# Row sums of the last 128 queries' exponentials: from TensorE and POOL to ScalarE, in every second head group

## The chip, the cores and the metric

The kernel runs on one core of a Trainium2 chip. The core has five engines that run side by side, each with its own queue that it works off in order: TensorE (PE in the profile: matrix products into PSUM), VectorE (DVE), ScalarE (ACT: functions of one element, here exponentials and copies), GpSimd (POOL) and SyncE (SP), which issues nearly all DMAs. They wait for each other through semaphores. PSUM has eight banks of 128 partitions by 512 floats.

The metric is the device time of one execution, in microseconds (us). Before the change it is 815.91 us, the median of three runs (814.34 to 816.56).

## The reference

The input x has 16 sequences of 512 tokens with 128 features. Each sequence goes through three layers with residual sums: half a feed-forward, causal attention, half a feed-forward.

```python
x = x + 0.5 * ffn(layernorm(x))
x = x + attention(layernorm(x))
x = x + 0.5 * ffn(layernorm(x))
# attention: 16 heads, keys and values through a latent of 32 columns
attn = softmax(where(key <= query, q @ k.T / 8, -inf))     # per head, 512 x 512
y = attn @ v ; out = y @ Wout
```

The softmax is what the change touches: for each head and query, exponentials of scores less their maximum, and the sum of these exponentials by which the output is divided.

## The kernel before

**Folded weights.** The weights of queries and keys are multiplied together beforehand, and those of values and outputs too. A head's scores are then products over 32 latent columns. Four heads make a head group (`HG = 4`), and a sequence has four groups. Groups are worked on in pairs; u = 0 and u = 1 name the first and the second group of a pair. The kernel has 32 pairs.

**Blocks and kinds.** The 512 queries are four blocks of 128. Because of the causal mask, query block i needs keys 0 to (i+1) x 128. Work is cut into kinds: kind 0 is query block 3 (the last 128 queries, all 512 keys), kind 1 is blocks 2 and 0, kind 2 is block 1 of both groups.

**Two score passes.** Each score is computed twice. The first pass (tile `sx`, queries on partitions, keys along the row) only gives the maxima: VectorE takes the largest of each row with its sign turned (`find_maxima`, line 642, tile `nmax`). POOL splits the maxima into three bf16 terms (`maxima`), TensorE turns them (`maxima_t`, tile `mt`), ScalarE copies them (`rows`). The second pass (tile `tx`, keys on partitions, queries along the row) starts from these maxima, adds the scores, and ScalarE takes exponentials into SBUF (`exponentials`, line 655, tiles `pt`). POOL sets what the causal mask forbids to zero (`zeros`, line 668).

**Steps.** A pair takes five steps, n % 5 = 0 to 4, in the order `STEP = ((0, 0), (1, 0), (2, 0), (1, 1), (0, 1))` of (kind, u). So step 4 does the first pass of kind 0 of the second group: the last 128 queries. In each step `burst` (line 673) runs the first pass of the current pair and the second pass of work six steps older (`LAG`), in two halves of two heads each that `merge` interleaves. The first half's stream is tx of heads 0 and 1 followed by sx of heads 0 and 1; beside it run sx of heads 2 and 3 and then tx of heads 2 and 3.

**Between the bursts** come products that are due:

- `values` (line 763): probabilities by latent, tile `o`, in step 4 for u = 0 and in step 1 for u = 1. ScalarE copies it to `osb` (line 773).
- `sums` (line 781): the exponentials by a matrix of ones, tile `s`, in step 0 for u = 0 and in step 2 for u = 1. ScalarE copies it (`ssb`, line 787), four DMAs write it to DRAM, one reads it back spread over 128 partitions; VectorE takes reciprocals, DMAs broadcast them, and POOL multiplies them onto `osb` (`normalise`, line 830).
- Before `sums`, POOL adds the exponentials of equal queries over the key blocks, so that TensorE streams fewer columns: `add_01` (line 738, two instructions of 768 columns), `add_2` (line 743) and `add_23` (line 748, for the last 128 queries alone).
- Work of neighbouring sequences: `front` (feed-forward `fp_a`, layer norm, transposition, keys `kt`, queries `qt`) and `tail` (output products `yp`, second feed-forward `fp_c`).

**What sets the order.** The program order on every engine is written by hand. `FRONT_STEPS`, `SECOND_STEPS` and `TAIL_STEPS` (lines 509 to 513) say at which step, counted from the first burst of the sequence, each piece of `front` and `tail` is issued; a sequence lasts ten steps. A value n - 0.25 stands right behind burst n and ahead of `values` and `sums`; a value n stands behind them; n - 0.5 stands ahead of the burst.

The entries of `FRONT_STEPS` are in order: statistics (two), loads of the next x, bias, turning z, feed-forward, statistics (two), layer-norm scaling, blocks back from DRAM, turning, keys `kt`, `kt` to DRAM, `kt` from DRAM, and the four query products.

**PSUM.** Two pools: four single banks (`bank`, tag tx) and two double banks (`two_banks`, tag sx), each used in turn. A burst takes all four single banks for tx and both double banks for sx. The products between bursts take their output through `take` (line 74): single banks for the first two, a double bank for a third.

```python
between.extend((bank, bank, lambda name: two_banks(name)[:, 0, :]))
```

A bank that is taken again must first have been read by whoever reads its old content.

Of the kernel before, what the change touches and what calls it, by code (L numbers as in the profile page):

```python
# [11 lines left out]
F32 = mybir.dt.float32  # L12
BF16 = mybir.dt.bfloat16
AF = mybir.ActivationFunctionType
# [4 lines left out]
P = 128  # L19
# [6 lines left out]
def macaron_kernel(  # L26
# [14 lines left out]
    nc = tc.nc  # L41
    B, L, D = x.shape
    LD = wkv.shape[1]
# [5 lines left out]
    HG = P // LD  # L49
# [6 lines left out]
    small = ctx.enter_context(tc.tile_pool(name="small", bufs=6))  # L56
# [3 lines left out]
    dram = ctx.enter_context(tc.tile_pool(name="dram", bufs=4, space=bass.MemoryType.DRAM))  # L60
# [5 lines left out]
    def bank(name):  # L66
        return ps_t.tile([P, 512], F32, tag="tx", name=name)

    def two_banks(name):
        return ps_s.tile([P, 2, 512], F32, tag="sx", name=name)  # L70
# [3 lines left out]
    def take(name):  # L74

        return between.popleft()(name) if between else bank(name)
# [429 lines left out]

    FRONT_STEPS = (-31, -30.5, -29, -28, -21, -19.25, -16, -16, -13, -10.5, -8, -4.25, -4, -3.5, -2, -1, 3, 4)
    SECOND_STEPS = (-9.5, -8.5, -7, -5.5, -5, -4.25, -4, -3.5, -2, -1, 3, 4)  # L510
    THIRD_STEPS = (-18.5, -18.5, -18.5, -18, -17.5, -17.25, -16, -16) + FRONT_STEPS[8:]
    FOURTH_STEPS = (-27, -26, -25.5, -25) + FRONT_STEPS[4:]
    TAIL_STEPS = (1.75, 2.5, 2.75, 3.5, 4.5, 7, 7, 7.75, 10.5)
# [102 lines left out]
    def probabilities(st, g, kind):  # L616

        if ("pt", kind, g) not in st:
            st["pt", kind, g] = probs.tile(
                [P, 4, HG, P], F32, tag=f"pt{kind}", name=f"pt{kind}_{st['b']}_{g}", bufs=1 if kind == 2 else 2  # L620
            )
        return st["pt", kind, g]

    def merge(*streams):

        at = [0.0] * len(streams)
        streams = [deque(seq) for seq in streams]
        while any(streams):
            k = min((k for k in range(len(streams)) if streams[k]), key=lambda k: at[k])
            for _ in range(2):  # L630
                dst, w, mv, first, last = streams[k].popleft()
                nc.tensor.matmul(dst, lhsT=w, rhs=mv, start=first, stop=last, skip_group_check=True)  # L632
            at[k] += math.prod(mv.shape[1:]) * (1 if mv.dtype == BF16 else 4)

    def find_maxima(sx, st, g, kind, u, pair):
# [9 lines left out]
        else:  # L645
            nc.vector.tensor_reduce(  # L646
                nmax[:, 1, heads, :], sx.rearrange("p k (u n) -> p k u n", u=2), AX.X, ALU.max, negate=True
            )

    def exponentials(tx, st, g, kind, u, pair):  # L650

        pt = probabilities(st, g + (u if kind < 2 else 0), kind)
        if isinstance(tx, list):
            for k in range(2):
                nc.scalar.activation(  # L655
                    pt[:, :, 2 * pair + k, :], tx[k].rearrange("p (b n) -> p b n", n=P), AF.Exp
                )
        else:
            nc.scalar.activation(
                pt[:, :, ts(pair, 2), :].rearrange("p b k n -> p k b n"),  # L660
                tx.rearrange("p k (b n) -> p k b n", n=P), AF.Exp,
            )
# [10 lines left out]
    def burst(n, s_at, t_at):  # L673


        s_kind, t_kind = STEP[n % 5], STEP[(n - LAG) % 5]
        ss, tt, s_seq, t_seq = [], [], [], []
        for k in range(2):
            if t_at:
                tt.append([bank(f"tx_{t_at[0]['b']}_{t_at[1]}_{n}") for _ in range(2)])  # L680

                t_seq.append(t_parts(tt[k], *t_at, *t_kind, k, k == 0 and (n - LAG) % STEPS == 0))
            ss.append(two_banks(f"sx_{s_at[0]['b']}_{s_at[1]}_{n}"))
            s_seq.append(s_parts(ss[k], *s_at, *s_kind, 1 - k, t_at is not None and k == 1))
        if t_at:
            merge(t_seq[0] + s_seq[1], s_seq[0] + t_seq[1])
        else:
            merge(s_seq[0])
            merge(s_seq[1])
        for k in range(2):  # L690
            find_maxima(ss[k], *s_at, *s_kind, 1 - k)
            if t_at:
                exponentials(tt[k], *t_at, *t_kind, k)
        if n % STEPS == STEPS - 1:
            maxima(*s_at)
        if t_at:
            zeros(*t_at, *t_kind)
# [33 lines left out]

    def add_01(st, g, k):

        if k == 0:
            st["b01", g] = probs.tile([P, 3, HG, P], F32, tag="b01", name=f"b01_{st['b']}_{g}")
        flat = [t.rearrange("p b k n -> p (b k n)")[:, ts(k, 6 * P)] for t in (
            st["b01", g], st["pt", 0, g][:, 1:], st["pt", 1, g][:, 1:])]
        nc.gpsimd.tensor_tensor(*flat, ALU.add)  # L738

# [4 lines left out]

    def add_23(st, g, u):

        both = st["b23", g + u] = probs.tile([P, HG, P], F32, tag="b23", name=f"b23_{st['b']}_{g + u}")
        nc.gpsimd.tensor_tensor(both, st["pt", 2, g][:, 2 + u], st["pt", 1, g + u][:, 0], ALU.add)  # L748

    def blocks(dst, w, tile_, start=False):  # L750

        for h in range(HG):
            mv = tile_[:, :, h, :]
            nc.tensor.matmul(  # L754
                dst[ts(h, LD), :].rearrange("p (b n) -> p b n", n=P), lhsT=w[h] if isinstance(w, list) else w,
                rhs=mv, start=start, stop=True, skip_group_check=True,
            )
# [17 lines left out]
    def sum_products(st, g, u, s_ps):  # L775
        g1, w = g + u, ones_f[:, :LD]
        blocks(s_ps[:, :P], w, st["pt", 0, g1][:, :1], start=True)
        blocks(s_ps[:, P:], w, st["b01", g1])
        blocks(s_ps[:, 384:], w, st["b23", g1].unsqueeze(1))

    def sums(st, g, u):

        b, g1 = st["b"], g + u
        s_ps = take(f"s_{b}_{g1}")
        sum_products(st, g, u, s_ps)
        ssb = act2.tile([P, L], F32, tag="ssb", name=f"ssb_{b}_{g1}", bufs=3)
        nc.scalar.copy(ssb, s_ps)
        sums_d = dram.tile([HG, L], F32, tag="sums", name=f"sums_{b}_{g1}")
        for h in range(HG):
            nc.sync.dma_start(sums_d[h : h + 1], ssb[h * LD : h * LD + 1, :])  # L790
        st["sums", g1] = small.tile([P, HG * L // P], F32, tag="sum", name=f"sum_{b}_{g1}")
        nc.sync.dma_start(st["sums", g1], sums_d.rearrange("h n -> (h n)").rearrange("(p n) -> p n", p=P))

# [71 lines left out]
    groups = [(states[b], g) for b in range(B) for g in range(0, NG, 2)]  # L865
    N = len(groups)
    STEPS = len(STEP)
# [57 lines left out]
    def parts(when):  # L925
        gens = todo.pop(when, ())
        for gen in gens:
            next(gen)
        return bool(gens)
# [7 lines left out]
    plan(first, 0, (0, 3, 4))  # L937
    plan(second, WINDOW, SECOND_STEPS)
    plan(second_normalised(), 0, (1.75, 2))
# [4 lines left out]
    for b in range(2, B):  # L944
        plan(front(b, states[b]), b * WINDOW, {2: THIRD_STEPS, 3: FOURTH_STEPS}.get(b, FRONT_STEPS))
    for b in range(B - 2):
# [4 lines left out]
    def due(n, k, lag=LAG):  # L951

        at_ = at(n, lag + k)
        return at_ if at_ and (n - lag - k) % STEPS == 0 else None

    def turn_maxima(n):
        if due(n, STEPS, 0):
            maxima_t(*due(n, STEPS, 0))

    def ready_work(n):  # L960

        if n < N * STEPS and due(n, 10):
            st, g = due(n, 10)
            normalise(st, g + 1)
        for u in range(2):
            if due(n, 2 + 3 * u):
                st, g = due(n, 2 + 3 * u)
                add_01(st, g + u, 0)
                add_01(st, g + u, 1)
            if due(n, 3 + 2 * u):  # L970
                add_2(*due(n, 3 + 2 * u), u)
            if due(n, 3 + u):
                add_23(*due(n, 3 + u), u)

    for n in range(N * STEPS):
        parts(n - 0.5)
        ready_work(n)
        burst(n, at(n), at(n, LAG))
        if due(n, 8):
            normalise(*due(n, 8))  # L980
        if n >= LAG:
            between.extend((bank, bank, lambda name: two_banks(name)[:, 0, :]))

        parts(n - 0.25)
        for u in range(2):
            if due(n, 3 + 2 * u):
                values(*due(n, 3 + 2 * u), u)
            if due(n, 4 + 2 * u):
                sums(*due(n, 4 + 2 * u), u)
        turn_maxima(n)  # L990
        if not parts(n) and n < LAG:
            keep_clock(4)
        for u in range(2):
            if due(n, 6 + 2 * u):
                st, g = due(n, 6 + 2 * u)
                reciprocals(st, g + u)
        between.clear()
# [4 lines left out]
    n = N * STEPS  # L1002
# [25 lines left out]
    o_ps, s_ps = bank("o_late"), bank("s_late")  # L1028
# [75 lines left out]
```

## Time and profile before

| | |
|---|---|
| median of three runs | 815.91 us |
| the profiled execution | 814.67 us, of which the span is 812.9 |
| granted TensorE clock in it | 0.989 of full speed, mean |
| one pair of groups (five bursts, 400.87 to 425.68) | 24.8 us |
| exponentials on ScalarE, line 655, 128x512 | 616 instructions, 598 ns each |
| maxima on VectorE, line 642, 128x1024 | 128 instructions, 1223 ns each |
| copies osb and ssb on ScalarE | 62 each, 585 and 586 ns |
| POOL additions, lines 738 / 743 / 748 | 126 / 63 / 63, 1821 / 1277 / 1277 ns |

The profile gives the busy time of each engine, rows of instruction groups by line (out<-in, how often, mean length, idle time before them and who ended it), a table of waits, a timeline of each engine, and the chain of work that ended last. In a timeline row the first number is the start in us from the beginning of the span, the second how long the (merged) instructions took together, and a bracket at the end is idle time of the engine before it and who ended that. In the table of waits the numbers are: us in total, how many times, and (where shown) the longest.

### The profile page before, as it was taken

What the parts mean: (1) busy time and instruction counts of PE and PEld (TensorE: products, weight loads), DVE (VectorE), ACT (ScalarE), POOL (GpSimd) and SP (SyncE); (2) the same over time, 40 slices, a digit from 0 to 9 for tenths busy, and PEclk for the clock granted to TensorE, in tenths of its full rate; (3) what the DMA queues carried; (4) which work ended last, traced back from release to release, by engine and by line L of the source; (5) the groups of instructions that cost most, each with busy time, mean ns of one, the idle gap of its engine ahead of it and who ended that gap; (6) DMA issues with size and microseconds to landing.
All of it is one profiled execution on the core that took longest, in us unless ns stands there. A gap on an engine that the chain in (4) does not pass through costs nothing.

```text
span 812.9 us, 35716 instructions
## 1 busy us (share of the span) xinstructions
PE 786.7 (97%) x15400; PEld 506.9 (62%) x15400; DVE 618.6 (76%) x1317; ACT 488.9 (60%) x971; POOL 678.4 (83%) x676
## 2 busy tenths in 40 slices
PE   7899999999999999999999999999999999999986
PEld 5456566675666657666566766666666766666554
DVE  7787887978779687877869787777878677686716
ACT  1237675757567565756667566666757566575651
POOL 1018898998998999898989989898999989998991
PEclk9989999999999999999999999999999999999998
DMA  5123122232422323332232323223222222212111
GB/s 138 27 57 68 32 72 60 69 71 73 95 61 69 77 66 80 76 82 60 70 84 61 84 69 82 67 67 88 56 64 67 51 72 69 59 46 59 41 41 30
DMA packets 171022, 54.01 MB, mean 66 GB/s; under 512 B 119512, under 2 KB 162680, under 8 KB 170864
## 3 DMA queue, kind: packets, MB, share of 16 engines
q1 hardware_dynamic: 170096, 51.44, 27.1%
q8 instruction: 120, 1.97, 1.0%
q14 instruction: 38, 0.31, 0.1%
q10 hardware_dynamic: 768, 0.30, 0.1%
HBM read 37.90 MB, written 13.80 MB: 64 GB/s over the span
## 4 chain that ended last, share of the span: by engine, by line
PE 75%; POOL 7%; DVE 7%; ACT 4%; DMA 4%; issue 2%; SPq 1%; DVEq 0%; POOLq 0%
PE sx L632 18%; PE tx L632 14%; PE o L754 14%; PE s L754 8%; PE yp L385 7%; PE qt_ps L385 6%; POOL b L738 4%; DVE nmax L642 3%; PE fp_a L385 2%; DMA rb<-recs 2%; ACT xn_b L355 2%; PE fp_c L385 2%; POOL ot L830 1%; DMA recs<-rec 1%; POOL b L743 1%
## 5 line engine op out<-in xcount | busy, mean ns | idle before, releaser
L642 DVE TENSOR_REDUCE nmax<-sx 128x2 f32<-128x768 f32 (+2 forms) x384 | 313.0, 863 | 106.4 <-PE tx L632 66.0
L655 ACT ACTIVATE pt<-tx 128x512 f32<-128x512 f32 x616 | 319.5, 598 | 85.5 <-PE tx L632 79.3
L632 PE MATMUL sx<-kt,qt 32*128 32x512 f32 (+3 forms) x2048 | 324.5, 444 | 0.0
L632 PE MATMUL tx<-qt,kt 32*128 32x512 f32 x1728 | 319.3, 469 | 0.0
L738 POOL TENSOR_TENSOR b<-pt,pt 128x768 f32<-128x768 f32 x126 | 226.8, 1821 | 0.5
L632 PEld LDWEIGHTS sx<-kt,qt 32*128 32x128 f32 x2048 | 176.7, 186 | 25.1 <-issue 1.0
L668 POOL TENSOR_SCALAR_AFFINE_SELECT pt<-pt 128x1024 f32<-128x1024 f32 (+1 forms) x162 | 145.2, 900 | 24.1 <-ACT pt L655 21.0
L754 PE MATMUL o<-pt,lat 128*32 128x512 f32 x1984 | 146.4, 435 | 0.9 <-POOL pt L668 0.9
L632 PEld LDWEIGHTS tx<-qt,kt 32*128 32x128 f32 x1728 | 131.5, 185 | 5.1
L754 PEld LDWEIGHTS o<-pt,lat 128*32 128x32 f32 x1984 | 62.5, 109 | 78.0 <-issue 57.7
L632 PE MATMUL tx<-rows,ones_u 6*128 6x512 bf16 (+1 forms) x988 | 109.9, 297 | 1.0 <-DVE wvo L292 0.5
L646 DVE TENSOR_REDUCE nmax<-sx 128x4 f32<-128x1024 f32 x64 | 75.4, 1219 | 32.1 <-PE tx L632 32.0
L830 POOL TENSOR_TENSOR ot<-osb,rb 128x512 f32<-128x512 f32 x62 | 79.0, 1274 | 20.3 <-DMA rb<-recs 20.3
L632 PEld LDWEIGHTS <-ones_u 6*128 6x128 bf16 x1024 | 43.2, 92 | 82.8 <-issue 70.1
L773 ACT COPY osb<-o 128x512 f32<-128x512 f32 x62 | 36.3, 585 | 92.3 <-PE o L754 92.3
L632 PE MATMUL sx<-eye_b,mask_w 32*128 32x64 bf16 (+1 forms) x2560 | 87.8, 183 | 2.9 <-DVE nmax L646 1.9
L632 PEld LDWEIGHTS <-mask_w 32*128 32x128 bf16 x2560 | 67.4, 92 | 33.0 <-issue 25.1
L743 POOL TENSOR_TENSOR b<-b,pt 128x512 f32<-128x512 f32 x63 | 80.5, 1277 | 5.1
L748 POOL TENSOR_TENSOR b<-pt,pt 128x512 f32<-128x512 f32 x63 | 80.4, 1277 | 0.1
L487 ACT COPY qt<-qt_ps 128x512 f32<-128x512 f32 x64 | 37.5, 586 | 53.8 <-PE qt_ps L385 53.8
L754 PE MATMUL s<-b,ones_f 128*32 128x384 f32 x992 | 65.1, 380 | 3.5 <-POOL b L743 3.5
L385 PE MATMUL qt_ps<-xnt_b_b,wqk 128*32 128x512 f32 x512 | 68.2, 605 | 0.1
(193 smaller groups left out, 813.8 us busy)
## 6 DMA issues: line engine op xcount, KB each, us to landing
rb<-recs SPq DMA_DIRECT2D x248, 64.0 KB
x<-in_x_dram SPq DMA_DIRECT2D x16, 256.0 KB
sums<-ssb SPq DMA_DIRECT2D x248, 2.0 KB
z_a<-in_x_dram SPq DMA_DIRECT2D x60, 64.0 KB
blocks_b<-xn_b SPq DMA_DIRECT2D x15, 256.0 KB
z_b<-blocks_b SPq DMA_DIRECT2D x60, 64.0 KB
kt<-kt_d SPq DMA_DIRECT2D x60, 64.0 KB
out_dram<-x_c SPq DMA_DIRECT2D x15, 256.0 KB
```

What stands on the lines that cost most here:

```text
L385: nc.tensor.matmul(dst[ts(h, LD), :], lhsT=w[:, ts(h, LD)], rhs=mv, start=start, stop=stop, skip_group_check=True)
L487: nc.scalar.copy(st["qt", g - g % 2][:, g % 2, :], mp)
L632: nc.tensor.matmul(dst, lhsT=w, rhs=mv, start=first, stop=last, skip_group_check=True)
L642: nc.vector.tensor_reduce(nmax[:, i, heads, u], sx[:, :, col : col + (i + 1) * P], AX.X, ALU.max, negate=True)
L646: nc.vector.tensor_reduce(nmax[:, 1, heads, :], sx.rearrange("p k (u n) -> p k u n", u=2), AX.X, ALU.max, negate=True)
L655: nc.scalar.activation(pt[:, :, 2 * pair + k, :], tx[k].rearrange("p (b n) -> p b n", n=P), AF.Exp)
L668: nc.gpsimd.affine_select(diag, diag, pattern=[[0, diag.shape[1]], [1, P]], compare_op=ALU.is_ge, fill=0.0, base=0, channel_multiplier=-1,)
L738: nc.gpsimd.tensor_tensor(*flat, ALU.add)
L743: nc.gpsimd.tensor_tensor(b01, b01, st["pt", 2, g][:, u], ALU.add)
L748: nc.gpsimd.tensor_tensor(both, st["pt", 2, g][:, 2 + u], st["pt", 1, g + u][:, 0], ALU.add)
L754: nc.tensor.matmul(dst[ts(h, LD), :].rearrange("p (b n) -> p b n", n=P), lhsT=w[h] if isinstance(w, list) else w, rhs=mv, start=start, sto ...
L830: nc.gpsimd.tensor_tensor(turned(st)[:, g, :], st["osb", g], st["rb", g], ALU.mult)
```

## The change

In step 4, behind the exponentials of the burst, ScalarE now also works on the first-pass scores of the second group's last 128 queries, which are still in the double banks `sx`. For each of the four heads one instruction takes exp(score - maximum) in place over the 512 keys, with the negated maximum as a per-partition bias, and its accumulator output gives the sum over the row (tile `own`). This is done in all pairs but the last (31 of 32). A new DMA, at the start of the step 2 that follows, writes these 128 x 4 sums into the sums' place in DRAM.

For these groups, `add_01` covers 512 columns per instruction in place of 768, `add_23` is left out, the product with ones covers queries 0 to 383, the copy `ssb` and its DMAs too.

Besides, pieces of `front` are moved: the feed-forward from step 1 to step 4 (-19.25 to -21.25), the keys from step 1 to step 4 (-4.25 to -6.25), and the four query products from steps 3, 4, 3, 4 to steps 1, 3, 1, 3.

```diff
-    FRONT_STEPS = (-31, -30.5, -29, -28, -21, -19.25, -16, -16, -13, -10.5, -8, -4.25, -4, -3.5, -2, -1, 3, 4)
-    SECOND_STEPS = (-9.5, -8.5, -7, -5.5, -5, -4.25, -4, -3.5, -2, -1, 3, 4)
+    FRONT_STEPS = (-31, -30.5, -29, -28, -22, -21.25, -16, -16, -13, -10.5, -8, -6.25, -5.5, -4.5, -4, -2, 1, 3)
+    SECOND_STEPS = (-9.5, -8.5, -7, -5.5, -5, -4.25, -4, -3.5, -2, -1, 1, 3)
...
+    def own_sums(sx, st, g, pair):
+        if ("own", g + 1) not in st:
+            st["own", g + 1] = small.tile([P, HG], F32, tag="own", name=f"own_{st['b']}_{g}", bufs=3)
+        for k in range(2):
+            nc.scalar.activation(
+                sx[:, k, :], sx[:, k, :], AF.Exp, bias=st["nmax", g][:, 3, 2 * pair + k, 1:2],
+                accum_out=st["own", g + 1][:, 2 * pair + k : 2 * pair + k + 1],
+            )
+
+    def own_sums_out(st, g):
+        sums_d = st["sums_d", g + 1] = dram.tile([HG, L], F32, tag="sums_0", name=f"sums_{st['b']}_{g}", bufs=3)
+        nc.sync.dma_start(sums_d[:, 384:].rearrange("h q -> q h"), st["own", g + 1])
...
             find_maxima(ss[k], *s_at, *s_kind, 1 - k)
             if t_at:
                 exponentials(tt[k], *t_at, *t_kind, k)
+        if n % STEPS == STEPS - 1 and s_at is not groups[N - 1]:
+            for k in range(2):
+                own_sums(ss[k], *s_at, 1 - k)
...
     def add_01(st, g, k):
+        n_ = (4 if ("own", g) in st else 6) * P
...
-        flat = [t.rearrange("p b k n -> p (b k n)")[:, ts(k, 6 * P)] for t in (
+        flat = [t.rearrange("p b k n -> p (b k n)")[:, ts(k, n_)] for t in (
...
     def add_23(st, g, u):
+        if ("own", g + u) in st:
+            return
...
         blocks(s_ps[:, :P], w, st["pt", 0, g1][:, :1], start=True)
+        if ("own", g1) in st:
+            blocks(s_ps[:, P:384], w, st["b01", g1][:, :2])
+            return
         blocks(s_ps[:, P:], w, st["b01", g1])
         blocks(s_ps[:, 384:], w, st["b23", g1].unsqueeze(1))
...
-        nc.scalar.copy(ssb, s_ps)
-        sums_d = dram.tile([HG, L], F32, tag="sums", name=f"sums_{b}_{g1}")
+        n_ = 384 if ("own", g1) in st else L
+        nc.scalar.copy(ssb[:, :n_], s_ps[:, :n_])
+        sums_d = st["sums_d", g1] if n_ < L else dram.tile([HG, L], F32, tag="sums", name=f"sums_{b}_{g1}")
         for h in range(HG):
-            nc.sync.dma_start(sums_d[h : h + 1], ssb[h * LD : h * LD + 1, :])
+            nc.sync.dma_start(sums_d[h : h + 1, :n_], ssb[h * LD : h * LD + 1, :n_])
...
         parts(n - 0.5)
+        if due(n, STEPS + 2, 0):
+            own_sums_out(*due(n, STEPS + 2, 0))
         ready_work(n)
```

## The prediction

> **What bounds the kernel now.** I read the page first: busy shares, then the chain that ended last, then the costliest groups.
>
> ```profile
> span 812.9 us, 35716 instructions
> PE 786.7 (97%) x15400; PEld 506.9 (62%) x15400; DVE 618.6 (76%) x1317; ACT 488.9 (60%) x971; POOL 678.4 (83%) x676
> PE 75%; POOL 7%; DVE 7%; ACT 4%; DMA 4%; issue 2%; SPq 1%; DVEq 0%; POOLq 0%
> ```
>
> TensorE (PE) holds three quarters of the chain. The product with ones (tile s, line 754) is 8% of it, so the change cuts at the engine that sets the end. A busy PE is not proof, so I looked at how one step follows the next in TensorE's timeline around 416 us (start, duration, what), from the last step of a pair of head groups (step 4) into the first step of the next pair (step 0):
>
> ```profile
> 416.61 0.23 PE L632 MATMUL tx<-rows,ones_u 6*128 6x128 bf16 x2
> ...
> 418.57 0.25 PE L632 MATMUL sx<-eye_b,mask_w 32*128 32x32 bf16 x8
> 418.86 2.36 PE L754 MATMUL o<-pt,lat 128*32 128x512 f32 x32
> 421.03 1.04 PE L385 MATMUL qt_ps<-xnt_b_b,wqk 128*32 128x512 f32 x8
> 422.01 0.39 PE L632 MATMUL tx<-rows,ones_u 6*128 6x512 bf16 x2
> ...
> 423.07 0.38 PE L632 MATMUL tx<-rows,ones_u 6*128 6x512 bf16 x2
> ```
>
> No row carries an idle bracket: burst (416.61 to 418.86), values o (to 421.03), query product (to 422.01), next burst, whose second half, tx of the other two heads, begins 1.06 us in. Time saved on TensorE is saved in full, and any wait put into this sequence is paid in full. ScalarE's timeline of the same stretch shows how much room there is:
>
> ```profile
> 418.02 2.06 ACT L655 ACTIVATE pt<-tx 128x512 f32<-128x512 f32 x4 [0.69 <-PE tx L632]
> 421.28 0.58 ACT L773 COPY osb<-o 128x512 f32<-128x512 f32 x1 [1.20 <-PE o L754]
> 422.14 0.58 ACT L487 COPY qt<-qt_ps 128x512 f32<-128x512 f32 x1 [0.27 <-PE qt_ps L385]
> ```
>
> The four exponentials end at 420.08, 1.22 us after the burst. Then ScalarE idles 1.20 us before it copies o, and 0.27 before it copies the query. The query copy ends at 422.72, only 0.35 us before 423.07. The average of 60% hides that: at this place ScalarE is the nearest thing behind TensorE.
>
> **The banks.** Four single banks rotate. A burst takes all four for tx; the next two products take the first two of them again; the next burst's second half takes these two back. So the second half of step 0 waits until both products of step 4 have been copied out. Today the second product is the query; after the change it is o.
>
> **Part 1, TensorE (gain).** A full sum product streams 128+384+128 = 640 columns per head. The changed one leaves out 128 of the 384 and the last 128, 256 columns. From the groups by line and form, the 62 sum products:
>
> ```profile
> L754 PE MATMUL s<-b,ones_f 128*32 128x384 f32 x496 | 51.6, 488 | 3.5 <-POOL b L743 3.5
> L754 PE MATMUL s<-b,ones_f 128*32 128x128 f32 x496 | 24.9, 273 | 0.0
> ```
>
> The page puts all of s<-b at 65.1 us; with overlap among forms I take 65.1/62 = 1.05 us as one product, which agrees with 424.24 to 425.35 in the timeline less the small product behind it. 256/640 of 1.05 is 0.42 us; 31 of 32 pairs have it: **-13.0 us**.
>
> **Part 2, POOL (mostly off the path).** Per pair one addition (line 748, 1277 ns) goes, and two of 768 columns (1821 ns) become 512 (1277, from line 748): 1.277 + 2 x 0.544 = 2.37 us, 73 us of POOL's 678. It is worth what TensorE waits for POOL's sums:
>
> ```profile
> PEld s L754 <- POOL b L743: 5.6, 8, 1.3
> PE s L754 <- POOL b L743: 3.5, 7, 1.0
> ```
>
> The two rows are mostly the same waits seen twice. Bounds 0 to 5.6; second groups, whose additions come straight after a late normalisation, have most: **-4 us**. The sum's copy (line 787) also shortens by a quarter of its elements, 0.11 us, felt only where ScalarE's layer-norm scaling follows it, about 15 times: **-1.5 us**. Gains together 18.5 us, 0.60 per pair.
>
> **Part 3, ScalarE (the cost).** Four activations are added per pair, behind step 4's exponentials and ahead of the copy of o. Each takes 512 elements, a per-partition bias and an accumulator output. None is in the trace, so I price its start-to-start pitch from rows that are. Exponentials: four in 2.06 us, last 0.60 long, so (2.06-0.60)/3 = 0.487. The layer-norm scalings, which have a per-partition operand, from ScalarE's timeline:
>
> ```profile
> 434.96 1.28 ACT L355 ACTIVATE xn_b<-x_a,r_w 128x128 f32<-128x128 f32 x4
> ```
>
> (1.28-0.39)/3 = 0.297 for 128 elements. An element costs 0.844 ns (1030 ns for 1024 against 598 for 512). Without elements the first leaves 0.055, the second 0.189: a per-partition operand adds 0.13. One added activation: 0.487+0.13 = **0.62 us**, if the sum comes free with it. That is the low end.
>
> Here a rule speaks against the change: the Trainium skill, "VectorE: DVE Perf Modes", section "Two Vector instructions with no wait between them", says that an operation with an accumulator output is two instructions, the main one and a read of the accumulator. It speaks of VectorE; no row here shows whether ScalarE does the same. By the rows alone the pitch is 0.62; with the rule, an instruction of almost no elements comes on top: 0.19 like an emptied scaling, up to 0.29, the distance from the small layer-norm exponential at 426.90 to the next instruction at 427.19. I take the rule for ScalarE too and the 0.19: **0.81 us**; ends 0.62 and 0.90.
>
> On a clock that starts at 416.61: the next ScalarE instruction can start at 419.97 (four pitches behind 418.02), +3.36. Four added ones, then the copy of o: ready at 3.36 + 4 x 0.81 + 0.59 = **7.19**. TensorE's side: the query leaves this place, and in turn the kt product (0.39 us, 428.03 to 428.42) or the first feed-forward (0.89, 403.22 to 404.11) comes ahead of o; both are copied by VectorE, free by then. So the burst 2.25, then 0.39 or 0.89, then o (about 2.22), and 1.06 into the next burst: bank wanted at **5.92 or 6.42**. Waits 1.27 and 0.77, mean 1.02; times 31: **+31.6 us**.
>
> The skill's page "PSUM — Partial Sum Buffer", section "Summary: rules for kernel authors", says to evacuate promptly because the memory is tight. It points at the sx banks, which the change does hold longer: the first until 3.36 + 1.62 = 4.98 (wanted at 4.86 or 5.36), the second until 6.60 (wanted at 5.92 or 6.42). By that hold alone the wait would be 0.68 or 0.18, mean 0.43, 13 us, and the kernel 5 us faster. The copy of o stands behind the same instructions and frees its bank 0.59 later, so it decides.
>
> **Part 4, moves and DMA (nothing).** Query products go from steps 3 and 4 to steps 1 and 3; step 1 then has values and query, as step 4 has today without a wait. Their sum on TensorE is unchanged. The kt transfer goes out one to one and a half steps earlier, behind nothing that is late. The new DMA writes 512 single elements, at the start of step 2. Its data are more than a step old, so SP does not wait. SP's z_a loads, also 512 pieces each, take 0.56 us to issue (2.22 for four); behind it stand the sums' DMAs, which wait for ScalarE anyway. 170096 packets took 27.1% of 16 engines' 812.9 us, 20.7 ns each; 512 of them are 0.66 us spread over 16 engines. If that cover were gone, the read-back of the sums would be late by that 0.66 us; normalisation on POOL would see it, and POOL has gained 2.4.
>
> **Sum.** 31.6 - 18.5 = +13.1 us. Against the profiled execution's 814.67 that is 827.8; the median shown is 1.24 above that execution, so **829 us**. With x the pitch, the mean wait is zero-cost only where it is under 0.60, at x = 0.70.
>
> **Rivals.**
> 1. *ScalarE's queue into the bank of o* (forecast; x from 0.72 to 0.90): 817 to 840, 829 at 0.81. For: no idle time on TensorE to hide in, ScalarE's in-order queue. Against: the pitch is pieced together. 0.52.
> 2. *The sum comes nearly free* (faster). Same place, pitch under 0.70, the point from which it decides; at 0.62 the waits are 0.51 and 0.01, 8 us, against 18.5: 805.5. For: ScalarE's rows show start-to-start far under duration, and the added ones write PSUM, which no row here does. Against: the rule above. 0.32.
> 3. *The accumulator drains the engine*: each activation must end (0.73 us) before its read starts, pitch over 0.90: 840 and more. For: the small layer-norm pair at 426.56 and 426.90 runs without overlap, because one needs the other. Against: nothing reads the sums at once. 0.11.
> 4. *A draw*: pitch 0.69 to 0.71, 815.9. 0.05.
>
> About 0.3% (2.4 us) is what a measurement of this kernel can tell from no change. Rivals 1 and 3 make slower 0.63, rival 4 same 0.05, rival 2 faster 0.32. The forecast's own range is 817 to 840. Leaving out a tenth at each end, 804 to 841 takes in both ends of the pitch.
>
> **What would show it.** In the changed trace: at step 4, added activations with a pitch near 0.81 and a second small instruction behind each; a TensorE gap of about 1 us in the middle of step 0's burst released by the copy of o (line of osb), longer in the pairs with kt than in those with feed-forward; sum products of second groups 0.42 us shorter; POOL's busy time down 73 us and no wait of s for b. If the wait is released by the added activations themselves, the sx banks decide and rival 2's sums apply. I am wrong if the pitch is under 0.70, or if step 0 shows no gap.

## The result, and the profile after

The changed kernel takes 944.13 us (938.41 to 948.23) against 815.6 (the kernel before, with a fourth run): a ratio of 1.157, 95% interval 1.1493 to 1.1648. It is some 129 us slower where 13 were forecast, and far outside the range of 804 to 841. Times here and below are medians of fast runs; one run of this kernel (953.55) and two of a_scatter, over 1.5% above the fastest of their kernel, are left out as slow. The profiled execution took 944.13 us, its span is 942.4.

From the page of the changed kernel, busy time and then the chain:

```profile
PE 840.7 (89%) x15152; PEld 520.6 (55%) x15152; DVE 614.8 (65%) x1317; ACT 573.2 (61%) x1219; POOL 607.3 (64%) x645
PE 54%; ACT 14%; issue 6%; DVE 5%; DMA 5%; POOL 4%; another core or an unknown queue 4%; SPq 2%; DVEq 0%; POOLq 0%; ACTq 0%
```

TensorE falls from 97% of the span to 89%, although hardly anything else is busier in share: ScalarE goes from 60 to 61%, and VectorE and POOL fall. So no engine took over as the bound. In the chain ScalarE grows from 4 to 14%, which the forecast would explain, and "issue" (an engine that waits for nothing the profile shows) from 2 to 6%; an unknown queue at 4% is new. TensorE's busy time even rose by 54 us with less work to do: the mean granted clock is 0.941 in place of 0.989.

The pauses have a place. These are SyncE's rows around one step 2 of the changed kernel (start, time to issue, line, what):

```profile
465.60 0.71 SPq L662 DMA_DIRECT2D sums<-own  x1
466.40 1.19 SPq L814 DMA_DIRECT2D sums<-ssb  x4
474.67 0.35 SPq L816 DMA_DIRECT2D sum<-sums  x1
```

and these of the kernel before:

```profile
412.36 1.12 SPq L790 DMA_DIRECT2D sums<-ssb  x4
414.45 0.35 SPq L792 DMA_DIRECT2D sum<-sums  x1
```

The new DMA goes out at 465.60, the four rows of sums right behind it at 466.40, and SyncE can read the sums back only at 474.67, 8.3 us behind the start of these rows. Before the change the same read-back followed 2.1 us behind. In the table of waits of SyncE's queue, first of the changed kernel, then of the kernel before (total us, times, longest):

```profile
SPq L816 <- DMA sums<-ssb: 172.7, 77, 7.7
```

```profile
SPq L792 <- DMA sums<-ssb: 53.7, 77, 1.1
```

The table of windows of the changed kernel shows what the rest of the core does meanwhile (window, then busy us of PE, PEld, DVE, ACT, POOL, the granted clock, the DMA engines' busy share, GB/s):

```profile
463.00:468.00 5.00, 5.00 (x140) 3.92 (x135) 3.91 (x12) 2.58 (x5) 5.00 (x5) 1.00 0.73 140
468.00:473.00 5.00, 3.81 (x62) 1.96 (x51) 1.48 (x7) 0.58 (x1) 4.92 (x5) 1.00 0.04 2
473.00:478.00 5.00, 4.34 (x42) 1.79 (x45) 3.88 (x12) 3.87 (x9) 1.95 (x7) 0.80 0.05 7
```

In the middle window the DMA engines move nearly nothing (2 GB/s after 140), and with them TensorE's weight loads, VectorE and ScalarE dry up. In the third the mean granted clock is 0.80; looked at by the us, it is 1.00 while TensorE stands half idle, and 0.50 three us later:

```profile
473.00:474.00 1.00, 0.51 (x8) 0.36 (x10) 0.00 (x0) 0.00 (x0) 0.69 (x1) 1.00 0.00 0
476.00:477.00 1.00, 1.00 (x8) 0.27 (x4) 1.00 (x5) 0.97 (x4) 0.47 (x2) 0.50 0.19 26
```

It stays at 0.50 until 479. The product of values that runs just then takes 3.89 us, where one took 2.36 before:

```profile
475.33 3.89 PE L774 MATMUL o<-pt,lat 128*32 128x512 f32 x32 [0.15 <-ACT pt L669]
```

This stretch is not the only one. Read packet by packet, the trace has 31 new DMAs; in the 14 us behind each, the longest time in which no packet starts on any of the 16 DMA engines is 5.1 us in the median. ScalarE's timeline of the changed kernel, of the same stretch, holds both the pause and the added work:

```profile
474.10 2.06 ACT L669 ACTIVATE pt<-tx 128x512 f32<-128x512 f32 x4 [4.11 <-remote]
476.03 0.70 ACT L655 ACTIVATE sx<-sx,nmax 128x512 f32<-128x512 f32 x1
476.60 0.23 ACT L655 ACTIVATION_READ_ACCUMULATOR sx<-sx,nmax 128x1 f32 x1
476.86 0.66 ACT L655 ACTIVATE sx<-sx,nmax 128x512 f32<-128x512 f32 x1
...
478.34 0.66 ACT L655 ACTIVATE sx<-sx,nmax 128x512 f32<-128x512 f32 x1
...
479.27 0.58 ACT L793 COPY osb<-o 128x512 f32<-128x512 f32 x1
```

It idles 4.11 us in front of the exponentials, released by no engine that the profile can name. Then come the added activations, each with an accumulator read behind it: four starts from 476.03 to 478.34 are a pitch of 0.77 us, forecast 0.81. The copy of o stands behind them as forecast. What was forecast is there; what makes the time is something else.

### The profile page after: what moved, and what is told of

It reads as the page before. It is cut to its first block, busy times and chain, and to the rows that moved or that the text cites. A ratio compares the mean times of both kernels' runs of the same rounds, so it can differ in the third digit from the quotient of the medians.

```text
span 942.4 us, 35459 instructions
## 1 busy us (share of the span) xinstructions
PE 840.7 (89%) x15152; PEld 520.6 (55%) x15152; DVE 614.8 (65%) x1317; ACT 573.2 (61%) x1219; POOL 607.3 (64%) x645
## 4 chain that ended last, share of the span: by engine, by line
PE 54%; ACT 14%; issue 6%; DVE 5%; DMA 5%; POOL 4%; another core or an unknown queue 4%; SPq 2%; DVEq 0%; POOLq 0%; ACTq 0%
PE sx L632 13%; PE tx L632 12%; PE o L774 9%; ACT pt L669 6%; PE yp L385 6%; PE qt_ps L385 5%; PE s L774 5%; ACT sx L655 4%; DVE nmax L642 2%; DMA recs<-rec 2%; DMA rb<-recs 2%; PE fp_a L385 2%; POOL b L756 1%; PE fp_c L385 1%
## 5 line engine op out<-in xcount | busy, mean ns | idle before, releaser
L669 ACT ACTIVATE pt<-tx 128x512 f32<-128x512 f32 x616 | 324.1, 599 | 123.5 <-PE tx L632 77.8
L632 PE MATMUL tx<-qt,kt 32*128 32x512 f32 x1728 | 345.0, 492 | 10.6 <-issue 10.5
L632 PE MATMUL sx<-kt,qt 32*128 32x512 f32 (+3 forms) x2048 | 347.8, 462 | 1.8 <-issue 1.8
L756 POOL TENSOR_TENSOR b<-pt,pt 128x768 f32<-128x768 f32 (+1 forms) x126 | 192.5, 1549 | 0.5
L774 PE MATMUL o<-pt,lat 128*32 128x512 f32 x1984 | 155.5, 453 | 3.7 <-issue 1.6
L632 PEld LDWEIGHTS tx<-qt,kt 32*128 32x128 f32 x1728 | 140.1, 194 | 21.6 <-issue 17.2
L632 PE MATMUL tx<-rows,ones_u 6*128 6x512 bf16 (+1 forms) x988 | 122.1, 305 | 26.8 <-ACT qt L487 11.2
L854 POOL TENSOR_TENSOR ot<-osb,rb 128x512 f32<-128x512 f32 x62 | 78.9, 1272 | 78.4 <-DMA rb<-recs 64.6
L655 ACT ACTIVATE sx<-sx,nmax 128x512 f32<-128x512 f32 x124 | 82.2, 663 | 3.5 <-DVE nmax L642 1.3
L385 PE MATMUL yp<-wvo,ot 128*32 128x128 f32 x1920 | 67.7, 288 | 12.8 <-issue 11.7
L385 PEld LDWEIGHTS yp<-wvo,ot 128*32 128x32 f32 x1920 | 55.5, 115 | 23.2 <-issue 16.3
```

What stands on the lines that cost most here:

```text
L385: nc.tensor.matmul(dst[ts(h, LD), :], lhsT=w[:, ts(h, LD)], rhs=mv, start=start, stop=stop, skip_group_check=True)
L655: nc.scalar.activation(sx[:, k, :], sx[:, k, :], AF.Exp, bias=st["nmax", g][:, 3, 2 * pair + k, 1:2], accum_out=st["own", g + 1][:, 2 * pa ...
L669: nc.scalar.activation(pt[:, :, 2 * pair + k, :], tx[k].rearrange("p (b n) -> p b n", n=P), AF.Exp)
L774: nc.tensor.matmul(dst[ts(h, LD), :].rearrange("p (b n) -> p b n", n=P), lhsT=w[h] if isinstance(w, list) else w, rhs=mv, start=start, sto ...
L854: nc.gpsimd.tensor_tensor(turned(st)[:, g, :], st["osb", g], st["rb", g], ALU.mult)
```

## The experiments

Two theories stood at the start. **D**: the new DMA holds up all DMA traffic, sums and instruction fetch included. **Q**, the forecast: ScalarE's queue in front of the copy of o. Later came a third, **R**, about POOL's queue. The median of the kernel before lies between 816.0 and 817.3 us in these comparisons.

### The DMA alone, and in other forms

All of these are the kernel before plus one DMA per pair at the place of the new one, from or into a tile that nobody uses.

```diff
+        if due(n, STEPS + 2, 0) and due(n, STEPS + 2, 0) is not groups[N - 1]:
+            spare_out(n)
...
+    # a_scatter
+    nc.sync.dma_start(there[:, 384:].rearrange("h q -> q h"), spare4)       # there: [4, 512]
+    # a_rows: there is [128, 4]
+    nc.sync.dma_start(there, spare4)
```

> The kernel before, plus only the new DMA: 512 single floats from a constant tile into the same places of a spare DRAM tile, at the start of step 2, in 31 pairs; nothing waits for it. Theory D (these four-byte writes hold up all other DMA traffic, the engines' instruction fetch included, for some 7 us each): 3 to 4 us lost per pair, 905 to 940 us. Theory Q (the forecast: ScalarE's queue in front of the copy of o makes the loss): no more than 3 us over the kernel before, 813 to 819.

Measured: 945.67 us (942.92 and 948.42), ratio 1.158 (1.1535 to 1.1626), a little more than D had. The DMA alone, with no work added to any engine and nobody waiting for it, costs as much as the whole change.

> The same, but the 2 KB go out as 128 rows of 16 bytes, side by side in the spare tile. Theory D: the number of small writes into the same lines is what costs, so this is close to the kernel before, 813 to 822 us. A rival of it (any DMA issued at this place of SyncE's queue costs): as slow as the scattered one, 900 us and more.

Measured: 816.35 us, ratio 0.9999 (0.9987 to 1.001). The same 2 KB at the same place in 16-byte rows are free. So it is not the DMA, nor its place in SyncE's queue; it is its form.

```diff
+    # a_apart: there is [128, 4, 128], one float in 512 bytes
+    nc.sync.dma_start(there[:, :, 0], spare4)
+    # a_half: two heads
+    nc.sync.dma_start(there[:2, 384:].rearrange("h q -> q h"), spare4[:, :2])
+    # a_actq: as a_scatter, on ScalarE's queue
+    nc.scalar.dma_start(there[:, 384:].rearrange("h q -> q h"), spare4)
+    # a_read: the other way
+    nc.sync.dma_start(here, spare_d.rearrange("h q -> q h"))
```

> The kernel before plus 512 single-float writes per pair as in a_scatter, but each lands 512 bytes from the next one in the spare DRAM tile. If what costs is that 128 writes fall into the same 512-byte stretch of DRAM and queue up there (theory D-line): near the kernel before, 813 to 825 us. If each single-float write to DRAM costs by itself wherever it lands (theory D-piece): as slow as a_scatter, 930 to 960 us.

Measured: 817.28 us, ratio 0.9998 (0.9985 to 1.0011). 512 single floats, each 512 bytes from the next, are free.

> As a_scatter, but only two of the four heads: 256 single floats. Theory D: the hold-up of some 7 us becomes 3.5; what is lost falls by more than half if the engines have a few us of instructions in hand (840 to 870 us), by half if they have none (880 us). A fixed cost of such a DMA, whatever its length, would leave 940 us.

Measured: 945.01 us, ratio 1.1566 (1.1516 to 1.1615). Half the floats cost as much as all, which neither form of D's expectation had. It is what was named for a fixed cost of such a DMA; a_quarter below tells the two apart.

> As a_scatter, but issued from ScalarE's DMA queue. If the hold-up lies in the DMA engines or in the memory, which all queues share (theory D): 930 to 965 us, and SyncE's sum DMAs still land late. If only DMAs behind it in the same queue are held up: under 830 us.

Measured: 1014.03 us, ratio 1.2459 (1.2356 to 1.2563). Another queue is no way out; it is worse than the 930 to 965 that D had. Here ScalarE issues the DMA too, so the extra loss is not assigned. That SyncE's sums still land late (longest wait 6.2 us in its table), and its keys, which also go through DRAM, too (longest wait 11.0, against 2.5 before), agrees with D.

> The other direction: the kernel before, plus 512 single floats per pair read from a spare DRAM tile, with the same stride, into a 128 x 4 tile in SBUF that nobody uses. If the write to DRAM is what is slow: 813 to 822 us. If 512 pieces of four bytes are slow in either direction: 900 us and more.

Measured: 817.32 us, ratio 1.0011 (0.9998 to 1.0023). Reading 512 single floats that lie side by side is free.

```diff
+    # a_quarter: 32 queries
+    nc.sync.dma_start(there[:, 384:416].rearrange("h q -> q h"), spare4[:32, :])
+    # a_perm2: spare4 is [128, 4, 2], there [128, 4]
+    nc.sync.dma_start(there, spare4[:, :, 0])
```

> As a_scatter, but only the first 32 queries: 128 single floats, 32 in each of four 512-byte stretches. Halving the number of heads took nothing off the loss, so the writes into one stretch seem to queue behind each other while stretches go side by side (theory D-line). If the stretch is 512 bytes, the hold-up falls from some 7 us to a quarter, under 2 us, most of which the engines bridge: 816 to 845 us. If the queue forms on pieces of 64 bytes (16 floats, as many per piece here as in a_scatter), or if the cost is fixed per DMA: 930 to 955 us.

Measured: 837.11 us, ratio 1.0254 (1.0208 to 1.03), as D-line (writes into one stretch queue behind each other) with a stretch of 512 bytes has it. Together with a_half it points to what the hold-up follows: the number of writes into one run of neighbouring floats, not the number of runs. SyncE's longest waits for its rows of sums say the same; in turn two heads (a_half), 32 queries (a_quarter), and floats apart (a_apart):

```profile
SPq L792 <- DMA sums<-ssb: 153.4, 76, 7.3
```

```profile
SPq L792 <- DMA sums<-ssb: 88.8, 78, 3.2
```

```profile
SPq L792 <- DMA sums<-ssb: 54.1, 87, 1.1
```

Less the 1.1 us of the kernel before, 128 writes into a run hold for 6.2 us and 32 for 2.1: as an estimate, 48 and 66 ns per write, one after the other, or 43 from the difference (4.1 us for 96). The quiet time of the DMA engines, taken as in the changed kernel, goes the same way: 4.8 us in a_half, 2.4 in a_quarter, 1.6 in a_apart.

But a_rows also writes 32 rows into each 512 bytes and is free. That left open whether separate writes queue up, or whether it matters that neighbouring floats come from different partitions.

> The kernel before plus 512 single floats per pair, as many as in a_scatter and 128 in each 512-byte stretch too, but laid out as in a_rows: the four floats of a partition lie together in DRAM (they lie apart in SBUF, so that each is a write of its own). If it is the number of separate writes into one stretch: as slow as a_scatter, 930 to 960 us. If it is that neighbouring floats come from different partitions: near the kernel before, 813 to 825.

Measured: 933.51 us, ratio 1.1422 (1.1279 to 1.1564). In a_perm2 every byte lands where it does in a_rows, from the same partition; only it is written by 512 writes in place of 128. So it is the separate writes into one stretch that make the hold-up. (With 32 rows of 16 bytes per 512 bytes a_rows holds nothing that shows, and with 32 single floats a_quarter does. Whether the unit is 512 bytes or less, and why 16 bytes are that much better, is not settled.)

### The rest of the change without that DMA

c_turn keeps the change but hands ScalarE's sums to TensorE, which turns them into the free quarter of the bank of sums.

```diff
-        if due(n, STEPS + 2, 0):
-            own_sums_out(*due(n, STEPS + 2, 0))
...
             blocks(s_ps[:, P:384], w, st["b01", g1][:, :2])
+            for h in range(HG):
+                nc.tensor.matmul(s_ps[ts(h, LD), 384:], lhsT=st["own", g1][:, h : h + 1].to_broadcast([P, LD]),
+                                 rhs=ident, start=False, stop=True, skip_group_check=True)
...
-        n_ = 384 if ("own", g1) in st else L
+        n_ = L
```

(so the copy `ssb` and its DMAs cover all 512 columns again)

> The changed kernel without the scattering DMA: TensorE multiplies ScalarE's sums with the identity (four products of 128 columns) straight into the free last quarter of the bank of sums, and the copy and the four row DMAs take all 512 columns as before. Theory D: the loss goes and ScalarE's queue is left: with the pitch of 0.77 us seen in the changed kernel's trace a wait of 0.86 per pair, 27 us, less 13 for the product, plus 6.6 for the turning, less 4 for POOL: 832 us (822 to 842). Theory Q as the whole cause: it stays at 930 to 950.

Measured: 831.12 us, ratio 1.0177 (1.0162 to 1.0192). The DMA's loss is gone, and the wait that the forecast named appears in c_turn: in the waits, and in the middle of a step 0 (from its first row to the last shown, the start of the next burst). The kernel before has neither, see 422.01 and 423.07 in the prediction.

```profile
PE tx L632 <- ACT osb L793: 9.2, 17, 0.5
```

```profile
430.92 0.39 PE L632 MATMUL tx<-rows,ones_u 6*128 6x512 bf16 x2
...
432.96 0.37 PE L632 MATMUL tx<-rows,ones_u 6*128 6x512 bf16 x1 [0.54 <-ACT osb L793]
...
435.57 0.70 PE L632 MATMUL tx<-qt,kt 32*128 32x512 f32 x2
```

The row of waits counts only what the profile sees as idle. From the starts of the bursts in TensorE's timeline, step 0 lasts 4.65 and 4.03 us in c_turn (pairs with kt and with feed-forward) against 3.68 before: waits of 0.97 and 0.35, mean 0.66.

That the time falls within a microsecond of the 832 is partly luck. The sum took a wait of 0.86 per pair, 27 us, where 0.66 make 20; and it left out a wait of the feed-forward that the moves bring (6.2 us in all, see below). The two nearly cancel.

own_unused has the moves and the added activations but drops their sums; sums and additions are as before.

> The kernel before with the moved pieces and the added activations, whose sums nobody uses; sums, additions and DMAs as before. It prices ScalarE's part alone. Theory D: 0.86 us per pair at the pitch of 0.77, so 815 + 27 = 842 us (830 to 850). Theory Q as the whole cause: 930 us or more.

Measured: 839.9 us, ratio 1.0292 (1.0271 to 1.0313). Next, the moves alone:

```diff
-    FRONT_STEPS = (-31, -30.5, -29, -28, -21, -19.25, -16, -16, -13, -10.5, -8, -4.25, -4, -3.5, -2, -1, 3, 4)
+    FRONT_STEPS = (-31, -30.5, -29, -28, -22, -21.25, -16, -16, -13, -10.5, -8, -6.25, -5.5, -4.5, -4, -2, 1, 3)
```

(with `SECOND_STEPS` likewise)

> The kernel before with only the moved pieces of the front (new FRONT_STEPS and SECOND_STEPS). Theory D and theory Q alike: the moves are free, 813 to 820 us. Were they to cost (theory M), part of the 24 us of own_unused would show here: 825 to 840 us.

Measured: 826.47 us, ratio 1.0111 (1.0064 to 1.0158). Neither D nor Q had this: alone, the moves cost 10 us. Their waits:

```profile
POOL ot L830 <- DMA rb<-recs: 42.9, 29, 2.9
PEld s L754 <- POOL b L743: 13.3, 16, 1.3
PEld fp_a L385 <- ACT pt L655: 6.2, 13, 0.5
```

The first two were 20.3 and 5.6 us before. POOL stands at the normalisation of the second group until the divisors (rb) are back from DRAM, and behind it in POOL's queue stand the additions for the next sum product. The third is new: the feed-forward, now right behind the burst of step 4, wants a bank whose exponentials are not finished. These 10 us are not simply a part of own_unused's 24: there the step 0 is longer, and TensorE's wait for POOL's sums is 3.0 us against 13.3 here, while the feed-forward's stays (5.9).

### Out of ScalarE's queue, and out of POOL's

c_turn_osb lets VectorE copy o in step 4.

```diff
-            nc.scalar.copy(st["osb", g + u], o_ps)
+            (nc.scalar.copy if u else nc.vector.tensor_copy)(st["osb", g + u], o_ps)
```

> c_turn, with VectorE in place of ScalarE copying o of the first group (step 4), so that this copy no longer stands behind the added activations. Theory Q for what is left in c_turn: the bank of o is free early, and the wait is that for the second sx bank, free at 3.36 + 4 x 0.77 = 6.44 against 5.92 or 6.42, mean 0.27 in place of 0.86: 18 us less than c_turn's 831, so 813 us (808 to 819). If the wait is not the copy of o: 828 to 833.

Measured: 830.75 us, ratio 1.0188 (1.0127 to 1.0249): nothing gained, though the four runs spread from 827.33 to 837.61, and the profiled one is the slowest. And yet step 0 fell as worked out, from 4.65 and 4.03 to 4.16 and 3.68. What was gained there went in the step of the second sum product (the one without an output product), which grew from 3.27 to 4.36 us (mean of 15). The waits of c_turn_osb:

```profile
POOL ot L859 <- DMA rb<-recs: 90.2, 29, 6.2
PEld s L774 <- POOL b L761: 16.7, 15, 3.8
```

TensorE gets to its sum product sooner, the divisors' round trip through DRAM doesn't get shorter, and POOL's additions wait behind it. This is theory R. A second way to carry the sums gave the same in stronger form: rows of 16 bytes out, then eight small reads back.

> The changed kernel with VectorE copying o in step 4, and ScalarE's sums written as 128 rows of 16 bytes (free in a_rows) and read back in the order needed by four small reads of single floats (free in a_read); the other sums are read back by four reads of 24 rows. No turning on TensorE, which is 6.6 us less than c_turn_osb: 806 us (801 to 813), 1% under the kernel before. Against it: SyncE issues seven more small DMAs per pair, some 2 us, ahead of the reciprocals; if POOL's normalisation comes late by that, 815 to 830.

Measured: 840.75 us, ratio 1.0286 (1.0236 to 1.0337), worse even than the 815 to 830 that was named against it.

R is tested by moving one instruction: the normalisation of the second group goes behind the additions of its step.

```diff
     def ready_work(n):
-        if n < N * STEPS and due(n, 10):
-            st, g = due(n, 10)
-            normalise(st, g + 1)
         for u in range(2):
...
+        if n < N * STEPS and due(n, 10):
+            st, g = due(n, 10)
+            normalise(st, g + 1)
```

> The kernel before, with the normalisation of second groups (step 1) put behind POOL's additions of that step in POOL's queue in place of ahead of them. Theory R: the waits of TensorE for POOL's sums go, at most 5.6 us: 809 to 815 us. If the place in the queue doesn't matter: 814 to 819.

Measured: 813.0 us, ratio 0.9949 (0.9932 to 0.9966). TensorE's wait for POOL's sums falls from 5.6 to 1.3 us:

```profile
PEld s L754 <- POOL b L743: 1.3, 1, 1.3
```

> The moved pieces alone, with the normalisation behind the additions. Of the moves' 10 us, the step behind the second sum product (4.11 against 3.80 us, and 5.36 against 5.23) should come back under theory R, 0.4 us per ten steps or 7 us; the feed-forward's step (5.80 against an expected 5.41) should stay: 817 to 821 us. If the moves cost by themselves: 824 to 828.

Measured: 816.18 us, ratio 0.9999 (0.9983 to 1.0015): all that the moves cost at the second sum product comes back, and the feed-forward's step stays at 5.80. Against before_late, the same order without the moves, they still cost 3 us.

> c_turn_osb with the normalisation behind the additions. Theory R: the 1.3 us per ten steps that step 2 had grown come back, 21 us off 831: 810 us (806 to 817). If what c_turn_osb lost lies elsewhere (VectorE's longer queue): 826 to 834.

Measured: 818.0 us, ratio 1.0028 (1.0016 to 1.004). The step of the second sum product is back at 3.27 us; POOL's wait for rb falls from 90.2 to 3.5 us. 13 us came back where 21 were expected. The 21 had been read in the profiled execution of c_turn_osb, which took 837.61, and were taken off the median of 831; from one profiled execution to the other it is 19.6 us. Step 0 keeps its 4.16 (the wait for the sx bank, as worked out) and the feed-forward's step its 5.86.

So R holds in the three kernels where it was tried, and it points to a version: no moves, both products of step 4 copied by VectorE, the normalisation late.

```diff
-            nc.scalar.copy(st["qt", g - g % 2][:, g % 2, :], mp)
+            (nc.vector.tensor_copy if g % 2 else nc.scalar.copy)(st["qt", g - g % 2][:, g % 2, :], mp)
```

(on top of turn_osb_late, with the old `FRONT_STEPS` and `SECOND_STEPS`)

> ScalarE's sums turned on TensorE, the old steps, VectorE copying both products of step 4 (o of the first group and the query), the normalisation behind the additions. ScalarE's last added activation ends at 6.44 on the clock of the prediction, where TensorE asks for the bank at 5.40 + 1.06 = 6.46: no wait. TensorE's 6.4 us and POOL's waits of some 5 us are gained: 805 us (801 to 811). If VectorE's two more copies make its maxima late: 815 to 825.

Measured: 808.82 us, ratio 0.9903 (0.9877 to 0.9928): faster than both kernels, by 4 us than before_late, and inside the 801 to 811 of the expectation. How much of these 4 us comes from the sums and how much from the copies moved to VectorE was not tried. Step 0 is at 3.68 us, as without the added activations. Busy times from its page:

```profile
PE 783.6 (97%) x15400; PEld 507.5 (63%) x15400; DVE 646.1 (80%) x1380; ACT 543.1 (67%) x1156; POOL 607.1 (75%) x645
```

TensorE is at 97% again, with ScalarE and VectorE fuller and POOL lighter. The last try was to save the turning as well:

> turn_old_late, with the turning on TensorE replaced by the DMAs of w_rows_osb (128 rows of 16 bytes out, four small reads of single floats and four of 24 rows back). If these DMAs are hidden: 6.6 us less than 808.8, so 802 us (799 to 806). If seven more small DMAs per pair make the divisors late, so that POOL's normalisation, now behind the additions, still holds up what follows: 810 to 825.

Measured: 845.92 us, ratio 1.0378 (1.0342 to 1.0415): a miss, slower than either case. SyncE's small DMAs stand ahead of the reciprocals, and the same wait is back, now at the normalisation of the first group in step 4, which was not moved:

```profile
POOL ot L866 <- DMA rb<-recs: 101.7, 30, 6.5
```

## Why the prediction was wrong

**The step that failed** is in part 4, "Moves and DMA (nothing)": 20.7 ns for each of 512 packets, "0.66 us spread over 16 engines". The DMA costs 129 us by itself (a_scatter), 4.2 per pair, and the read-back of the sums comes up to 6.6 us late (longest wait 7.7 against 1.1) where part 4 had 0.66 at most. The packet price was not too low: in the trace of the changed kernel a packet of four bytes occupies its engine for 9 ns in the median, as in a_apart, which costs nothing. What was missing is the time until such writes have landed, in which the other traffic stands. No DMA of the kernel before puts many single floats side by side into DRAM: the nearest in number of pieces, z_a, writes into SBUF, and the nearest in size, the rows of sums, are 2 KB long. I had priced the issue and the movement and not the landing, and gave the unknown no upper end. The Trainium skill, "DMA: Bandwidth & Descriptors", section "Specifications", notes that transfers under 512 bytes make the DMA engine read, modify and write. That would make writes into one stretch wait for each other, and it fits that floats far apart are free; why rows of 16 bytes are free too it does not say. The runs show the hold-up and not its cause.

**How the hold-up reaches TensorE.** Two ways show. The rows of sums land late, so the divisors do too, POOL stands (its wait for rb is 64.6 us in total in the changed kernel, 20.3 before), and the additions behind it can come late for TensorE. And the engines pause with nothing to wait for (ScalarE's 4.11 us above) while the DMA engines stand still.

The first way shows alone in a_quarter, where the hold-up is short: the granted clock stays at 0.990, "issue" in the chain is 3%, and TensorE waits for POOL (5.6 us before):

```profile
PEld s L754 <- POOL b L743: 19.5, 16, 2.4
```

In the changed kernel, where POOL has less to add, the same wait is 3.6 us, so there it is mainly the pauses and what follows them. For a_half, which has the 15400 products of the kernel before, the sizes can be told in part: the span is 127 us longer, and 49 of these are products that took longer (TensorE busy 835.9 against 786.7, at a mean clock of 0.955); the rest is idle time.

The pauses look like instructions that are not there yet. The page of the changed kernel, and under it that of the kernel before (packets, MB, share of the 16 engines' span), has the instruction queue slower with the same bytes:

```profile
q8 instruction: 119, 1.95, 1.2%
```

```profile
q8 instruction: 120, 1.97, 1.0%
```

1.2% of 16 x 942.4 is 181 us, 1.0% of 16 x 812.9 is 130. The longest of its packets takes 4.0 us against 1.6 before, and all 21 that take over 2 us start within 9 us of a new DMA. Against it as the whole cause: a_quarter has 18 such packets, and none of its waits lacks a releaser (the profile's "remote"). So that the pauses are a wait for instructions is argued and not shown.

**Point by point.**

- *What bounds it*: right as far as tried. The waits that were put on TensorE lengthened its steps; turn_old_late, faster, has TensorE at 97% again.
- *Part 1, -13 us*: right in size. The step with output product and second sum is 4.80 us in the changed kernel (median) against 5.23, 0.43 less where 0.42 was forecast.
- *Part 2, POOL*: busy time fell by 71 us (73 forecast). In c_turn TensorE's wait for the additions is nearly gone (0.2 us of 5.6), so the -4 us are about right; the place in POOL's queue was worth 3 us even before (before_late).
- *Part 3, ScalarE*: the mechanism is right and the price half too high. The pitch is 0.77, with a read of the accumulator behind each activation, as the rule for VectorE suggested, and 0.19 to 0.23 us long where 0.19 was taken. The wait is 0.66 per pair against 1.02; it is the copy of o that ends it, and the hold of the second sx bank comes next (c_turn_osb), both as ordered in the prediction.
- *Part 4, moves*: wrong as well, by 10 us where they stand alone. I had checked the banks in step 1 and TensorE's sum. I had not asked what a shorter step 4 does to POOL, whose additions stand behind a DMA round trip that does not shrink (theory R), nor whether the feed-forward finds a finished bank right behind the burst. Its wait stays in moves_late (5.8 us in all).
- *Rivals*: none of the four had the DMA. That the sign was right is luck as far as the changed kernel goes: nearly all of its loss is the term put at nothing. In c_turn, the change without that DMA, the forecast's mechanism is there, but of its 15 us some 6.6 are put to the turning (an estimate) and some 6 to the feed-forward's wait. With the wait as measured, the forecast's own sum is 20 less 18.5: near a draw, not 13 us slower.

## What to carry to other kernels

Price a DMA by how it lands: count how many separate writes fall into the same few hundred bytes of DRAM, and where the trace has no row of that form, give it an open upper end rather than the mean packet. Turn such data on chip, or leave gaps; writing rows (a_rows) and scattering on the reading side (a_read) cost nothing here, but more small DMAs in an issuing queue that is already full do (rows_old_late). And where TensorE is the bound, look at what stands behind a DMA round trip in another engine's queue, before counting a saving: here one instruction moved behind the additions was worth 3 us in the kernel before and 13 in a changed one.

## What the runs showed of the hardware

- Single-float writes into one run of DRAM behave as if served one after another, some 43 to 66 ns each (an estimate from 6.2 us for 128 and 2.1 us for 32). Runs go side by side: two cost what four cost (945.01 and 945.67 us). The same floats 512 bytes apart (817.28), as 16-byte rows (816.35), or read (817.32) cost nothing that can be measured.
- Such a hold-up stops the DMA traffic of other queues as well: issued from ScalarE it makes SyncE's sums and keys late (longest waits 6.2 and 11.0 us, against 1.1 and 2.5), and packets of the instruction queue take up to 4.0 us in place of 1.6. Their recorded time on the DMA engines does not show it: a four-byte packet takes 9 ns (median) whether it holds up or not.
- An activation with an accumulator output is two instructions on ScalarE, the second 0.19 to 0.23 us; with a per-partition bias, over 512 elements in place in PSUM, the pair has a pitch of 0.77 us.
- TensorE's granted clock was 1.00 during a pause and 0.50 from 476 to 479, some 3 us behind it; over the changed kernel it is 0.941 on average. In a_half 49 of 127 us are products that ran slower.
